# A bias inside 64-token blocks, moved from TensorE matmuls to a POOL multiply behind exp, with the value matmuls one step later

## Chip, core and metric

The kernel runs on one core of a Trainium2 chip. The metric is the device time of one execution in microseconds (us), lower is better. The kernel before takes 1742.46 us (median of 3 runs, 1741.09 to 1747.34).

## What is computed

Four stages in float32 on x of 8 batches x 512 tokens x 128, each followed by a residual sum and a layernorm: an attention with 16 heads of width 8 and a linear distance bias (the first attention), a gated feed-forward with blockwise FP4 rounding of tokens and weights, a second attention without bias, and a local-attention transformer of two layers. The change is in the first attention:

```
slopes = 2 ** (8 * arange(0, -H, -1) / H)                 # one per head, H = 16
scores = einsum('bhqd,bhkd->bhqk', q, k) / sqrt(Hd)
bias   = -slopes[:, None, None] * abs(pos[None, :] - pos[:, None])
probs  = softmax(scores + bias[None], axis=-1)
out    = einsum('bhqk,bhkd->bhqd', probs, v)
```

The second attention has the same form without `bias`.

## The kernel before

**Units and steps.** `attention` is used for both attentions, with `alibi` true for the first. Its work is cut into 32 units, 4 groups of 4 heads in each of 8 batches. A unit has 8 steps in the first pass and 8 in the second; the second pass of a unit lies LAG = 16 steps behind its first. A step `s` thus does one step of the first pass of unit `s // 8` and one of the second pass of unit `(s - 16) // 8`, each for one block of 128 tokens and one pair of heads.

- First pass, in `step`: two matmuls `s_ps` of 128 queries against 512 keys, and VectorE's maximum over the keys into `m` (both heads in one instruction). Two score tiles rotate (pool `p_s`).
- At step 1 of the following unit `shift` transposes the maxima, ScalarE copies them to `mt`, and POOL issues two DMAs that write them into row 63 of q. In this way the second pass subtracts them inside its matmul.
- Second pass, in `step`: two matmuls `t_ps` of 128 keys against 512 queries; ScalarE's exp makes `e` from each (scale: the slope of the head). `t_ps` comes from a pool of three PSUM banks, `p_t`, which transposes and projections share. `e` tiles rotate, 11 of them.
- `values`, two groups of four matmuls for each key block (`part` 0 and 1 are the two halves of the queries), adds up `av` in the only bank of `p_av`. After the last group ScalarE copies `av` to `avs`.
- `divide` transposes `avs` into `o_ps` and divides by the denominator on VectorE. Once in a batch `end_o` and `end_y` transpose and project the output (`ot_ps`, `y_ps`), VectorE makes sum and statistics, and `layernorm` runs six instructions on POOL.

**The bias.** Rows 32 to 47 of the operands q and k carry, for each 64-token block, a signed distance, so that the matmul itself gives the linear bias. For a query in the block of the key this has one sign only, so `corrected` adds, inside the diagonal 64x64 blocks, twice the missing distance: four small bf16 matmuls of the constants `sel` and `tri` into the same bank. It does so in each step for the first pass and for the second.

**What sets the order.** All instructions around the change are kept in program order on their engines. `later(s, f)` puts a function behind `step` number `s`; functions of one step run in the order in which they were put. The due times that matter, with `z` the first step of the second pass of a unit: `values` of block `blk` and half `part` at `z + 2 * blk + 3 + part` (line 413), `divide` at `z + 12` (line 410), `end_o` at `z + 15`, `end_y` with `layernorm` at `z + 18`, `shift` at `n * 8 + 9`. For the next batch's operands `begin_x` runs at 10 steps before a batch's first step, `begin_qk` at 8 and 6 before it (ScalarE's `x`, then POOL's cast and subtraction that make `parts`, then DMAs on the SyncE queue to DRAM and back), `begin_v` and `with_bias` at 20 steps after it. Counted in steps from a batch's start, 58 is thus the one in which `end_y` of that batch, `layernorm` and the second `begin_qk` of the batch after next fall together, in this order. From step 62 on, `quantized_tokens` rounds that batch for the feed-forward (VectorE, POOL and ScalarE).

**Loads.** Weights of the later stages come in `load_weights`, at step 64 of the first attention, among them the local attention's `wqkv_s` (1.5 MB) on the SyncE queue.

Of the kernel before, what the change touches and what calls it, by code (L numbers as in the profile page):

```python
# [9 lines left out]
F32 = mybir.dt.float32  # L10
F32R = mybir.dt.float32r
BF16 = mybir.dt.bfloat16
I32 = mybir.dt.int32
AF = mybir.ActivationFunctionType
ALU = mybir.AluOpType
# [3 lines left out]
P = 128  # L19
B, S, D = 8, 512, 128  # L20
# [5 lines left out]
C_ID, C_TRI, C_SEL, C_MASK0, C_MASK, C_ROT = 0, 128, 256, 512, 640, 768  # L26
# [25 lines left out]
def body(ctx, tc, x, consts, rows, wa0, wa1, acols, bo, wf, wqkv, wo, w1, w2, cols, b2r, qs, ks, out):  # L52
    nc = tc.nc
    pe, dve, act_, pool_ = (Kept(tc, e) for e in (nc.tensor, nc.vector, nc.scalar, nc.gpsimd))
# [5 lines left out]
    cst = outer.tile([P, C_ROT], F32, name="cst")  # L60
# [1 line left out]
    rowq = outer.tile([16, S], F32R, name="rowq")  # L62
    rowk = outer.tile([17, S], F32R, name="rowk")
    sel = outer.tile([P, 2 * P], BF16, name="sel")
    tri = outer.tile([P, P], BF16, name="tri")
    wa = [outer.tile([P, W_ALL], F32, name=f"wa{i}") for i in range(2)]
    wqkv_s = outer.tile([P, 2, 3 * INNER], F32, name="wqkv_s")
    wo_s = outer.tile([P, 2, 4, D], F32, name="wo_s")
# [29 lines left out]
        dve.tensor_copy(rowk, raw[:, 1, :])  # L98
    dve.tensor_tensor(qb, acol[:, :, 0], acol[:, :, 1], ALU.mult)
    dve.tensor_copy(sel, cst[:, C_SEL : C_SEL + 2 * P])  # L100
    dve.tensor_copy(tri, cst[:, C_TRI : C_TRI + P])

    def load_late():
        for b in range(2, B):
# [2 lines left out]
    def load_weights():  # L107
        held(out=cst[:, C_MASK0:C_ROT], in_=consts[:, C_MASK0:C_ROT])
        held(out=wa[1], in_=wa1)
        held(out=wqkv_s, in_=wqkv.rearrange("l p f -> p l f"))  # L110
        held(out=wo_s, in_=wo.rearrange("l (c p) d -> p l c d", p=P))
        held(out=w1_s, in_=w1.rearrange("l p f -> p l f"))
        held(out=w2_s, in_=w2.rearrange("l (c p) d -> p l c d", p=P))
        held(out=cols_s, in_=cols)
# [137 lines left out]
    def attention(li, alibi, qs_, ks_, va, batch, late=None, spare=None, alone=0):  # L252
# [7 lines left out]
        with ExitStack() as st:  # L260
# [1 line left out]
            bank = lambda name: p_t.tile([P, S], F32, tag="t", name=name)  # L262
            begun = len(batch)
            batch += [{} for _ in range(B - begun)]
            work = crow = None

            def hold_o(h):
                h["o"] = work.tile([P, NT, P], F32, tag="o", name="o", bufs=3)
# [2 lines left out]
                for c in range(NT):  # L271
                    pool_.tensor_tensor(xs[:, b * NT + c, :], xn[:, b * NT + c, :], crow, ALU.add)

            def corrected(ps, lo, at, stop):

                for a in range(2):
                    for j in range(2):
                        r = slice(64 * j, 64 * j + 64)
                        mm(
                            ps[j][:, lo + 64 * a : lo + 64 * a + 64], lhsT=sel[r, a * P : (a + 1) * P],  # L280
                            rhs=tri[r, at : at + 64], start=False, stop=stop and a == 1, skip_group_check=True,
                        )

            def step(u, i, v, k):


                if u:
                    blk, pp = i // 2, i % 2
                    p, lo = 2 * u["g"] + pp, (i // 2) * P
                    q, kk = qs_[u["b"] % 2], ks_[u["b"] % 2]  # L290
                    both = p_s.tile([P, 2, S], F32, tag="s", name="s_ps")
                    ps = [both[:, j, :] for j in range(2)]
                    for j in range(2):
                        r = slice(64 * j, 64 * j + 63)
                        mm(
                            ps[j], lhsT=q[r, p, lo : lo + P], rhs=kk[r, p, :], start=True, stop=not alibi,
                            skip_group_check=True,
                        )
                    if alibi:
                        corrected(ps, lo, 0, True)  # L300
                if v:
                    vp, vlo = 2 * v["g"] + k % 2, (k // 2) * P
                    q, kk = qs_[v["b"] % 2], ks_[v["b"] % 2]
                    ts = [bank("t_ps") for j in range(2)]
                    for j in range(2):
                        r = slice(64 * j, 64 * j + 64)
                        mm(
                            ts[j], lhsT=kk[r, vp, vlo : vlo + P], rhs=q[r, vp, :], start=True, stop=not alibi,
                            skip_group_check=True,
                        )  # L310
                if u:
                    if i == 0:
                        u["m"] = small.tile([P, 2, 2, NT], F32, tag="m", name="m")
                    dve.tensor_reduce(u["m"][:, :, pp, blk], both, AX.X, ALU.max)
                if v:
                    if alibi:
                        corrected(ts, vlo, 64, True)
                    for j in range(2):
                        e = work.tile([P, S], F32, tag="e", name="e", bufs=11)
                        act_.activation(e, ts[j], AF.Exp, scale=float(SLOPES[2 * vp + j]) if alibi else 1.0)  # L320
                        v["e"].append(e)

            def shift(u):

# [12 lines left out]
            def values(u, blk, part):  # L337

                if blk == 0 and part == 0:
                    u["av"] = p_av.tile([P, S], F32, tag="av", name="av")  # L340
                at = slice(part * S // 2, (part + 1) * S // 2)
                for r in range(4):
                    mm(
                        u["av"][32 * r : 32 * r + 32, at], lhsT=va[u["b"] % 2][:, blk, 4 * u["g"] + r, :],
                        rhs=u["e"][4 * blk + r][:, at], start=(blk == 0 and part == 0), stop=(blk == NT - 1), skip_group_check=True,
                    )
                if blk == NT - 1 and part == 1:
                    u["avs"] = work.tile([P, S], F32, tag="avs", name="avs")
                    act_.copy(u["avs"], u["av"])

            def divide(u):
# [38 lines left out]
                later(n * NU + 9, shift, units[n])  # L390

            def plan():
                nonlocal work, crow
                const, work = pool("ac", 1), pool("aw", 2)
                dram = pool("ad", 2, space=bass.MemoryType.DRAM)
                begin_x, begin_qk, load_qk, begin_v = operand_steps(
# [7 lines left out]
                for n in range(B * G):  # L404
# [2 lines left out]
                    later(z + 12, divide, units[n])  # L407
                    for blk in range(NT):
                        for part in range(2):
                            later(z + 2 * blk + 3 + part, values, units[n], blk, part)  # L410
                    if g == 0 and begun <= b + 1 < B:

                        early = max(s - 10, 8)
# [13 lines left out]
                if not begun:  # L427
                    begin_x(0, batch[0])
                    begin_qk(0, batch[0], 0, held)
                    begin_qk(0, batch[0], 1, held)  # L430
                    begin_v(0, batch[0])
                    for part in (slice(0, 2), slice(2, 4), 1):
                        load_qk(0, batch[0], 0, part, held)
                        load_qk(0, batch[0], 1, part, held_a)
# [710 lines left out]
    with tc.tile_pool(name="ops", bufs=1) as ops:  # L1145
# [27 lines left out]
        def first_spare(later, done, work, bank, mm, tr, p_s):  # L1173
            temps = lambda: [work.tile([P, S], F32, tag=t, name=t, bufs=1) for t in ("qy", "qm")]
            later(64, load_weights)
            for j in range(3):
                quantize_weights(later, 28 + 11 * j, j, temps, work, bank, tr)

# [53 lines left out]
def _constants():  # L1232
# [1 line left out]
    c = np.zeros((P, C_ALL), np.float32)  # L1234
    c[:, C_ID : C_ID + P] = p == f
    i = p % 64
    c[:, C_TRI : C_TRI + 64] = -2.0 * np.maximum(f[:, 0:64] - i, 0)
    c[:, C_TRI + 64 : C_TRI + P] = -2.0 * np.maximum(i - f[:, 0:64], 0)
    for a in range(2):
        c[:, C_SEL + a * P : C_SEL + (a + 1) * P] = f == 64 * a + i  # L1240
    seen = (f >= i) & (f <= i + 64)
# [16 lines left out]
    at, blk = np.arange(S) - S // 2, np.arange(S) // 64  # L1258
    rows = np.zeros((17, 2, S), np.float32)
    for n in range(8):  # L1260
        sign = np.where(blk <= n, 1.0, -1.0)
        rows[n, 0], rows[8 + n, 0] = blk == n, (blk == n) * at
        rows[n, 1], rows[8 + n, 1] = sign * at, -sign
    rows[16, 1] = -1.0
# [56 lines left out]
```

## Time and profile before

| | us |
|---|---|
| median of 3 runs | 1742.46 |
| profiled execution, device time | 1744.98 |
| its span, first to last instruction | 1743.1 |
| first attention, from its first matmul of scores | about 28 to 505 |
| first feed-forward | about 505 to 620 |
| second attention, the start overlapping the stage before | about 620 to 1020 |
| last stage | about 1020 to 1743 |

Busy time by stage, in us:

| stage | length | TensorE | VectorE | ScalarE | POOL | granted clock |
|---|---|---|---|---|---|---|
| 28 to 505 | 477 | 466.6 | 360.7 | 324.4 | 125.2 | 0.96 |
| 505 to 620 | 115 | 86.6 | 97.1 | 55.7 | 76.0 | 0.96 |
| 620 to 1020 | 400 | 390.4 | 339.5 | 312.3 | 113.7 | 0.98 |

A profile row names engine, line of the kernel, operation, tiles (written <- read), shapes and count. PE is TensorE's matmul, PEld its weight load, DVE VectorE, ACT ScalarE, SP SyncE. Many instructions are issued through helpers, so that they all bear the helper's line (L48, L258, L259); the tile names tell them apart. In square brackets behind a row is how long the engine stood idle before it, and what it waited for. The granted clock is TensorE's, as a share of full speed. Matmuls are pipelined: the distance between two starts says more than the length of one.

### The profile page before, as it was taken

The page shows a single profiled execution, that of the slowest core. Times are in us where ns is not written, and L with a number is a line of the kernel's source. Part 1 is how long each engine was busy: PE and PEld are TensorE (multiplying, and loading weights), DVE is VectorE, ACT ScalarE, POOL GpSimd, SP SyncE. Part 2 cuts the span into 40 slices and gives each one's busy share as a digit, 9 for nine tenths or more (in the row PEclk, how much of TensorE's full clock was granted, in tenths as well). Part 3 has the DMA queues.
Part 4 walks back from the last instruction along what each step waited for, and adds up shares of the span by engine and source line. Part 5 has one row for each costly group of instructions (what it writes and reads, how often), then busy time and mean ns, then how long its engine had stood idle before and what let it go on. Part 6 is the DMA issues. An engine that isn't in the chain of part 4 may idle for free.

```text
span 1743.1 us, 42097 instructions
## 1 busy us (share of the span) xinstructions
PE 1637.8 (94%) x16304; PEld 950.2 (55%) x16305; DVE 1381.6 (79%) x2209; ACT 1257.5 (72%) x2996; POOL 911.9 (52%) x974
## 2 busy tenths in 40 slices
PE   4999999999988789999999989999999999999995
PEld 2455555455546544444444446666766666666664
DVE  4688777878839888888888847788888888888873
ACT  1577777776764558878778867788887888888883
POOL 3223331332126741323222257888888888888873
PEclk7799999999999989999999999999999999999998
DMA  5735222321110234333323101111111111111110
GB/s 125 155 68 143 65 54 47 67 59 26 14 14 1 73 66 84 64 62 73 68 52 55 44 1 35 35 35 38 41 38 35 35 41 38 44 41 42 37 35 25
DMA packets 80777, 90.27 MB, mean 52 GB/s; under 512 B 46097, under 2 KB 58385, under 8 KB 76610
## 3 DMA queue, kind: packets, MB, share of 16 engines
q1 hardware_dynamic: 75504, 85.52, 23.2%
q8 instruction: 130, 2.13, 0.5%
q10 hardware_dynamic: 978, 1.52, 0.3%
q0 software_dynamic: 4096, 0.54, 0.3%
q14 instruction: 69, 0.57, 0.1%
HBM read 41.85 MB, written 18.87 MB: 35 GB/s over the span
## 4 chain that ended last, share of the span: by engine, by line
PE 77%; DVE 7%; ACT 6%; POOL 5%; issue 2%; DMA 2%; SPq 1%; DVEq 0%; POOLq 0%; ACTq 0%
PE av L258 15%; PE s_ps L258 12%; PE t_ps L258 9%; PE y_ps L645 5%; PE sp L645 4%; PE o_ps L645 3%; PE t_ps L645 3%; PE v_ps L645 3%; PE p_ps L645 2%; PE q_ps L645 2%; PE k_ps L645 2%; ACT e L48 2%; PE gp L645 2%; PE ap L645 2%; PE o_ps L259 2%
## 5 line engine op out<-in xcount | busy, mean ns | idle before, releaser
L48 DVE TENSOR_REDUCE m<-s_ps 128x2 f32<-128x1024 f32 x512 | 622.5, 1224 | 154.1 <-PE s_ps L258 148.9
L48 ACT ACTIVATE e<-t_ps 128x512 f32<-128x512 f32 x1024 | 556.3, 596 | 178.4 <-PE t_ps L258 170.1
L258 PE MATMUL av<-e,va 128*32 128x256 f32 x4096 | 328.1, 393 | 10.8 <-ACT avs L48 10.7
L258 PE MATMUL s_ps<-k,q 63*128 63x512 f32 x1024 | 265.3, 511 | 20.5 <-DMA q<-far 14.4
L48 POOL DMA_DIRECT2D q<-mt x128 | 68.9, 542 | 365.9 <-ACT mt L48 365.9
L258 PE MATMUL t_ps<-q,k 64*128 64x512 f32 x1024 | 248.1, 448 | 1.3 <-ACT e L48 1.3
L645 ACT ACTIVATE pw<-sp,m,was_v 128x128 f32<-128x128 f32 x512 | 227.6, 480 | 1.5 <-DVE m L645 1.0
L258 PEld LDWEIGHTS s_ps<-k,q 63*128 63x128 f32 x1024 | 99.8, 189 | 227.9 <-issue 151.3
L645 POOL TENSOR_TENSOR was_v<-was_v 128x16 f32<-128x16 f32 x64 | 187.6, 2931 | 5.3
L258 PEld LDWEIGHTS av<-e,va 128*32 128x32 f32 x4096 | 81.5, 108 | 100.5 <-issue 58.9
L258 PEld LDWEIGHTS t_ps<-q,k 64*128 64x128 f32 x1024 | 122.5, 189 | 22.7 <-ACT e L48 10.6
L645 POOL TENSOR_TENSOR pw<-pw,den 128x1024 f32<-128x1024 f32 x64 | 121.3, 1895 | 9.1 <-DVE den L645 9.1
L645 ACT ACTIVATION_READ_ACCUMULATOR pw<-sp,m,was_v 128x1 f32 x512 | 115.9, 226 | 0.0
L258 PEld LDWEIGHTS <-sel 64*128 64x128 bf16 x2048 | 67.3, 98 | 76.6 <-issue 53.3
L645 DVE TENSOR_REDUCE m<-sp 128x4 f32<-128x512 f32 x128 | 82.2, 683 | 21.9 <-PE sp L645 20.1
L48 POOL CAST parts<-x 128x512 fp32r<-128x512 f32 x32 | 19.5, 610 | 138.4 <-ACT x L48 138.4
L645 POOL TENSOR_TENSOR was_k<-was_k,was_q 128x512 f32<-128x512 f32 x64 | 88.0, 1376 | 6.1 <-DVE was_q L645 6.1
L645 ACT COPY v<-v_ps 128x512 f32<-128x512 f32 x64 | 37.6, 588 | 72.7 <-PE v_ps L645 72.7
L645 PEld LDWEIGHTS t_ps<-cst,was_k 128*128 128x128 f32 x512 | 59.7, 142 | 43.2 <-issue 22.4
L645 DVE COPY pT<-p_ps 128x512 f32<-128x512 f32 x128 | 79.8, 664 | 0.5 <-PE p_ps L645 0.5
L645 PEld LDWEIGHTS p_ps<-cst,pw 128*128 128x128 f32 x512 | 59.8, 141 | 33.0 <-issue 28.0
L645 DVE TENSOR_REDUCE was_v<-was_k 128x16 f32<-128x1024 f32 x64 | 77.0, 1204 | 0.0
(191 smaller groups left out, 3282.1 us busy)
## 6 DMA issues: line engine op xcount, KB each, us to landing
far<-parts SPq DMA_DIRECT2D x64, 256.0 KB
q<-far SPq DMA_DIRECT2D x248, 64.0 KB
k<-far SPq DMA_DIRECT2D x240, 64.0 KB
ve<-v SPq DMA_DIRECT2D x112, 128.0 KB
xn<-in_x SPq DMA_DIRECT2D x8, 256.0 KB
q<-mt POOLq DMA_DIRECT2D x128, 4.0 KB, 3.1
hn<-xs SPq DMA_DIRECT2D x16, 128.0 KB
hn<-xs SPq DMA_DIRECT2D x16, 112.0 KB
```

Of the source, the lines that this page charges most:

```text
L48: return lambda *a, **k: self.tc.keep_in_program_order(f(*a, **k))
L258: mm = lambda *a, **k: tc.keep_in_program_order(nc.tensor.matmul(*a, **k))
L259: tr = lambda *a, **k: tc.keep_in_program_order(nc.tensor.transpose(*a, **k))
L645: kept = lambda f: lambda *a, **k: tc.keep_in_program_order(f(*a, **k))
```

## The change

- The second pass has no corrections any more. Its `t_ps` takes no bias inside a 64-token block: `sign` in the constants is now 0 there.
- `e` becomes one tile for both heads, 6 of them. After the two exps POOL multiplies, in place, the 128 columns of the diagonal block in both heads by a table `near`, exp(-slope x distance) inside a 64-token block and 1 outside.
- `near` (16 heads x 128x128) is made at the start by 16 exps on ScalarE, ahead of the loads of the first batch's k on ScalarE's queue. It lies in the space of `wqkv_s`, whose load moves to step 282, behind the last second-pass step.
- The first pass keeps its four corrections, with one table `tri` of -distance for both sides of the diagonal.
- `values` is due one step later, in both attentions: `z + 2 * blk + 4 + part`. `avs` has one buffer instead of two.

```diff
-    tri = outer.tile([P, P], BF16, name="tri")
+    tri = outer.tile([P, 64], BF16, name="tri")
...
-    dve.tensor_copy(tri, cst[:, C_TRI : C_TRI + P])
+    for j in range(2):
+        r = slice(64 * j, 64 * j + 64)
+        dve.tensor_copy(tri[r], cst[r, C_TRI + 64 * j : C_TRI + 64 * j + 64])
...
-        held(out=wqkv_s, in_=wqkv.rearrange("l p f -> p l f"))
...
                         mm(
-                            ts[j], lhsT=kk[r, vp, vlo : vlo + P], rhs=q[r, vp, :], start=True, stop=not alibi,
+                            ts[j], lhsT=kk[r, vp, vlo : vlo + P], rhs=q[r, vp, :], start=True, stop=True,
                             skip_group_check=True,
                         )
...
                 if v:
+                    e = work.tile([P, 2, S], F32, tag="e", name="e", bufs=6)
+                    for j in range(2):
+                        act_.activation(e[:, j], ts[j], AF.Exp, scale=float(SLOPES[2 * vp + j]) if alibi else 1.0)
+                        v["e"].append(e[:, j])
                     if alibi:
-                        corrected(ts, vlo, 64, True)
-                    for j in range(2):
-                        e = work.tile([P, S], F32, tag="e", name="e", bufs=11)
-                        act_.activation(e, ts[j], AF.Exp, scale=float(SLOPES[2 * vp + j]) if alibi else 1.0)
-                        v["e"].append(e)
+
+                        at = e[:, :, vlo : vlo + P]
+                        pool_.tensor_tensor(at, at, near[:, 2 * vp : 2 * vp + 2, :], ALU.mult)
...
-                    u["avs"] = work.tile([P, S], F32, tag="avs", name="avs")
+                    u["avs"] = work.tile([P, S], F32, tag="avs", name="avs", bufs=1)
...
-                            later(z + 2 * blk + 3 + part, values, units[n], blk, part)
+                            later(z + 2 * blk + 4 + part, values, units[n], blk, part)
...
                     begin_v(0, batch[0])
+                    if alibi:
+
+                        near = wqkv_s.rearrange("p l f -> p (l f)")[:, 0 : 16 * P].rearrange("p (n f) -> p n f", n=16)
+                        for n in range(16):
+                            act_.activation(near[:, n, :], cst[:, C_TRI : C_TRI + P], AF.Exp, scale=float(SLOPES[n]))
...
             later(64, load_weights)
+            later(done(B - 1) - 4, lambda: held(out=wqkv_s, in_=wqkv.rearrange("l p f -> p l f")))
...
-    c[:, C_TRI : C_TRI + 64] = -2.0 * np.maximum(f[:, 0:64] - i, 0)
-    c[:, C_TRI + 64 : C_TRI + P] = -2.0 * np.maximum(i - f[:, 0:64], 0)
+    c[:, C_TRI : C_TRI + P] = np.where(p // 64 == f // 64, -np.abs(f - p), 0)
...
-        sign = np.where(blk <= n, 1.0, -1.0)
+        sign = np.sign(n - blk)
```

## The prediction

> **What bounds the kernel now.** I read the page first, for the busy shares and the chain that ended last. The core is busy on TensorE for 94% of the span, and 77% of the last chain is TensorE.
>
> ```profile
> PE 1637.8 (94%) x16304; PEld 950.2 (55%) x16305; DVE 1381.6 (79%) x2209; ACT 1257.5 (72%) x2996; POOL 911.9 (52%) x974
> PE 77%; DVE 7%; ACT 6%; POOL 5%; issue 2%; DMA 2%; SPq 1%; DVEq 0%; POOLq 0%; ACTq 0%
> ```
>
> Then the windows by stage (columns: window, its length, busy PE, PEld, DVE, ACT, POOL, granted clock, DMA share, GB/s). The first attention runs from about 28 to 505 us, the second from about 620 to 1020. In the middle of the first, TensorE has no idle time, VectorE is at 81% and POOL at 26%:
>
> ```profile
> 350.00:450.00 100.00, 98.88 (x1232) 50.74 (x1231) 80.91 (x102) 71.12 (x137) 26.00 (x38) 1.00 0.19 36
> ```
>
> Last, the timeline of TensorE, for one plain step of the first attention and one of the second, which has no bias and so no corrections (start, length, what):
>
> ```profile
> 214.03 0.49 PE L258 MATMUL s_ps<-k,q 63*128 63x512 f32 x2
> 214.36 0.23 PE L258 MATMUL s_ps<-tri,sel 64*128 64x64 bf16 x4
> 214.43 0.48 PE L258 MATMUL t_ps<-q,k 64*128 64x512 f32 x2
> 214.76 0.23 PE L258 MATMUL t_ps<-tri,sel 64*128 64x64 bf16 x4
> 214.92 0.64 PE L258 MATMUL av<-e,va 128*32 128x256 f32 x8
> 215.49 0.49 PE L258 MATMUL s_ps<-k,q 63*128 63x512 f32 x2
> ```
> ```profile
> 820.23 0.50 PE L258 MATMUL s_ps<-k,q 63*128 63x512 f32 x2
> 820.57 0.40 PE L258 MATMUL t_ps<-q,k 64*128 64x512 f32 x2
> 820.90 0.64 PE L258 MATMUL av<-e,va 128*32 128x256 f32 x8
> 821.47 0.50 PE L258 MATMUL s_ps<-k,q 63*128 63x512 f32 x2
> ```
>
> Starts count, not lengths, since matmuls overlap. First attention: 0.33 to the first pass's correction, 0.07 to the second pass, 0.33 to its correction, 0.16 to the values, 0.57 to the next step: 1.46 us. Second: 0.34, 0.33, 0.57: 1.24 us. A batch (32 steps) of the first takes 57.0 us (POOL's casts of `parts` at 188.65, 245.60, 302.56): 46.8 plain, the rest transposes, projections and short waits, all on TensorE. So TensorE sets the pace here, and a matmul less is time less, until something else is late.
>
> **Removed: the second pass's correction.** 4 matmuls in each of 256 steps: 0.16 each step by the rows, and the second attention confirms that the values then follow `t_ps` at 0.33. 256 x 0.16 = 41.0. About 8 of these steps run at a granted clock of 0.50 (54 to 66 us), where the same four cost about twice as much: 1.3 more. In the last 16 steps, without a first pass, exp paces (1.08 busy, 0.21 waiting for `t_ps`); there the wait goes, 0.05 a step more than counted: 0.8. Sum -43. The new step is 1.31 us; the maximum that VectorE takes in each is 1.23, so VectorE is next in line but not yet the bound.
>
> **Added: POOL's multiply**, 256 of 128x256 f32, both operands in SBUF. No such row; POOL's 128x128 takes 455 ns, its 128x384 840, its 128x512 1060 to 1376. Bounds 0.6 and 0.76; I take 0.66, between 128x128 and 128x384. That is 21 us a batch on an engine that has 15 of 57, so as a rate it is hidden. It lies behind exp and before the values three steps later: exp ends 1.93 us after its step's start, the values of a block's first half want it 0.74 into the third step after, 4.7 us from the start: 2.7 us of slack, of which 0.66 is the multiply. What counts is POOL's order. At the step that ends a batch (58 of each 32, y_ps), POOL's own queue has the layernorm and then the next operand's cast and subtraction:
>
> ```profile
> 307.48 0.24 POOL L48 TENSOR_SCALAR rstd<-stats 128x4 f32<-128x4 f32 x1 [1.96 <-DVE stats L48]
> 307.80 1.04 POOL L48 TENSOR_TENSOR rstd<-rstd,half 128x4 f32<-128x4 f32 x1
> 308.95 3.13 POOL L48 TENSOR_SCALAR xn<-xs,stats,rstd 128x128 f32<-128x128 f32 x4
> 312.04 0.60 POOL L48 CAST parts<-x 128x512 fp32r<-128x512 f32 x1
> 312.73 1.28 POOL L48 TENSOR_TENSOR parts<-x,parts 128x512 fp32r<-128x512 f32 x1
> ```
>
> It waits for `stats`, then runs 6.5 us to 314.0. The multiply of step 59 stands behind that. Moved to the new times (two corrections earlier, 0.32): `stats` at 307.16, POOL free at 313.7, multiply ready at 314.36, at the values with 0.1 of latency 314.45. TensorE is there as follows: step 59 starts at 306.70, 60 at 308.01, 61 at 310.32 (a transpose of 0.59 and the wait below, 0.40), 62 at 311.63, its values at 312.37. Wait 2.08 us, and everything on TensorE is queued behind it. Six batches have both pieces (0 to 5); batch 6 has no next operand and comes out even. +12.5.
>
> A rule of the Trainium skill bears on this wait. TensorE: Matmul & The Clock Gate (What's actually happening) says that the array falls to half clock after one idle window of about 3.4 us. The trace agrees at both ends:
>
> ```profile
> 512.51 2.60 PE L48 MATMUL gu<-wgu,xqT 128*128 128x352 f32 x8 [2.59 <-DVE h L473]
> ...
> 522.48 1.54 PE L473 MATMUL ht_ps<-cst,y 128*128 128x128 f32 x6 [3.69 <-POOL y L473]
> 523.81 4.49 PE L48 MATMUL gu<-wgu,xqT 128*128 128x352 f32 x8
> ```
>
> After 2.59 us idle eight matmuls took 2.60; after 3.69 they took 4.49, and the clock stood at 0.50 until 526. At 2.08 the row and the rule say no loss; past 3.4 the sum would be another one (below).
>
> **Moved: the values a step further behind, in both attentions.** Before, the copy of `av` (`avs`) was made at step 2 of a unit's 8, the next values waited for it in step 3, and the transposes of `divide` came a step later, free of it. Now the copy is at step 3 and `divide`, unmoved, is the first to want it in step 4. Now:
>
> ```profile
> 219.17 0.48 PE L258 MATMUL t_ps<-q,k 64*128 64x512 f32 x2
> ...
> 219.94 0.64 PE L258 MATMUL av<-e,va 128*32 128x256 f32 x8 [0.22 <-ACT avs L48]
> ```
>
> From `t_ps` to the values 0.77 instead of 0.49: 0.28 lost, 0.27 in the second attention; in three units of four (21 waits in 390 us), since the fourth has y_ps in that step. The chain of waits goes exp, `avs`, TensorE: 1.61 us from exp's start. After: exp starts 0.84 into step 3, so `avs` is there at 2.45; the transposes want it at 1.31 + 0.74 = 2.05: 0.40, in all four units. Second attention: 0.77 + 1.62 = 2.39 against 1.24 + 0.67 = 1.91: 0.48. A batch of the first: 4 x 0.40 - 3 x 0.29 = 0.73, of the second 4 x 0.48 - 3 x 0.27 = 1.11; times 8: 5.8 + 8.9 = +14.7. Exp and the next step's matmuls stand behind the same wait.
>
> **FFN tokens' quantization** (steps 63 to 68 of seven batches). VectorE gets 1.39 us there in one step and 0.68 in each of two others, besides 1.23 a step. At 1.46 a step it caught up within the two score buffers; at 1.31 it is late by about 0.65 a batch. ScalarE's 0.65 us `qm` pushes exp and thus `avs` by 0.2. Weight quantization adds about 1 in all. 7 x 0.85 + 1: +7. Here SBUF — State Buffer (Who interferes with whom) speaks against the change: a VectorE instruction with two SBUF inputs is shut out while POOL reads SBUF. Only the two 0.68 us instructions are such (most of their runs stand at 0.68, the longest at 1.55). Shut out by 0.66 each, a batch would lose up to 1.3 more, 9 in all; the maxima read PSUM and are not touched by that rule. I take none of it, as the two rarely meet, and keep 9 for the range.
>
> **Nothing:** 16 exps for the factors lie in ScalarE's gap from 16.05 to 24.16, while it waits to issue k's loads; at 0.3 each (the 16x128 cast takes 0.24) they need 5 of 8 us, and would cost any excess over 8. `tri` in two copies lies beside VectorE's start-up. The weight load of 1.5 MB leaves step 64 for the end: the SyncE queue issues nothing after it until 584.88 and DMA is at 0.00 from 510 to 560; uncovered it would be about 10 us at the 150 GB/s of the first slices. The e buffers (6 pairs for 11 singles) come free a matmul group before they are asked for, as before. The last unit waits for a multiply: +0.6.
>
> **Sum:** -43 + 12.5 + 14.7 + 7 + 0.6 = -8.2, against the profiled execution's 1745.0 (span 1743.1). The median of the runs is 1742.5, 2.5 under it, so 1734.
>
> **Rivals.** (1) The moved wait is absorbed: while TensorE stands, VectorE, which is almost as loaded, catches up, and later waits for it vanish. For it: weight loads of `s_ps` already wait 20.6 us for VectorE in the second attention. Against: a step with the wait is 1.51 against 1.24, all of it visible. 1734 - 14.7 = 1719; 18%. (2) The layernorm doesn't hold the values, since the copies go faster or the wait falls into another: 1734 - 12.5 = 1722; 12%. (3) Slower: the wait behind the layernorm passes 3.4 us and the clock falls. With a multiply of d us it is 2.08 + (d - 0.66) + 2(d - 0.66) - 0.26 (those of 57, 58 and 59; the first 0.26 hidden), 3.4 at d = 1.2. Then each of six batches loses 3.4 plus about 3.4 at half clock (7 us, as from 519 to 529): 41 instead of 12.5, time 1763; 7%. Against it: d would be that of 512 elements. (4) VectorE paces at once, the step stops at 1.39 instead of 1.31: 20 lost, 1754; 5%. That the change doesn't do what it says is excluded on TensorE: the matmuls are gone from the program.
>
> **Numbers.** The likeliest case, all four terms, has 58%, with 1723 to 1746 of its own. Half a per cent, about what a measurement of this kernel can tell from no change, is 8.7 us: faster ends at 1733.7. Half of the likeliest case and rivals 1 and 2 lie below; that gives 0.53, 0.35 and 0.12. Range 1715 to 1752.
>
> **What would show it.** `t_ps<-tri,sel` gone, step 1.31; POOL's multiply at 0.6 to 0.76; the values of step 62 waiting 2 us for POOL, six times; `o_ps` waiting for `avs` 0.4 to 0.5, 64 times; second attention longer by 9 us. Wrong if `o_ps` doesn't wait, if POOL waits spread over more steps than 62, or if the granted clock drops in the first attention.

## The result, and the profile after

The changed kernel takes 1748.16 us (median of 11 runs, 1742.29 to 1749.81); the kernel before took 1741.7 beside it (11 runs, 1739.4 to 1747.34). The ratio is 1.0032, with an interval of 1.0021 to 1.0043: 0.3% slower, where 0.5% faster was forecast. The profiled execution after took 1749.46 us, with a span of 1747.7. Below, one of the four executions of e10 is left out as slow: it took 6414 us at a mean granted clock of 0.23.

The page after, busy shares and the chain that ended last:

```profile
PE 1621.3 (93%) x15280; PEld 915.0 (52%) x15281; DVE 1391.9 (80%) x2210; ACT 1256.5 (72%) x3012; POOL 1096.1 (63%) x1230
...
PE 67%; DVE 10%; ACT 9%; POOL 8%; DMA 3%; issue 2%; SPq 0%; ACTq 0%; POOLq 0%; DVEq 0%
```

The 1024 matmuls are gone (16304 to 15280), but TensorE is only 16.5 us less busy, and its share of the last chain fell from 77% to 67%: VectorE, ScalarE and POOL took over. The window in the middle of the first attention (columns as before):

```profile
350.00:450.00 100.00, 95.61 (x1006) 42.58 (x1008) 83.26 (x103) 70.52 (x139) 67.57 (x97) 1.00 0.16 35
```

In the middle of the first attention TensorE now stands still for 4.4% of the time, against 1.1% before. Below, a "batch" is the distance between the starts of VectorE's maxima, 32 steps on. It was 57.0 us in the first attention and is 57.2; it was 50.1 in the second and is 51.2.

The plain step after, TensorE's timeline (start, length, what):

```profile
220.91 0.50 PE L259 MATMUL s_ps<-k,q 63*128 63x512 f32 x2
221.25 0.23 PE L259 MATMUL s_ps<-tri,sel 64*128 64x64 bf16 x4
221.32 0.48 PE L259 MATMUL t_ps<-q,k 64*128 64x512 f32 x2
221.73 0.64 PE L259 MATMUL av<-e,va 128*32 128x256 f32 x8
222.30 0.50 PE L259 MATMUL s_ps<-k,q 63*128 63x512 f32 x2
```

From `t_ps` to the values it is 0.41 us, not 0.33. The step is 1.39, not 1.31, with nothing waited for in it. Before, `t_ps`, its correction and the values took 0.33 + 0.16 = 0.49. So only 0.08 of the 0.16 came off.

The wait behind the layernorm, on TensorE (step 62 of the second batch):

```profile
192.64 0.50 PE L259 MATMUL s_ps<-k,q 63*128 63x512 f32 x2
...
193.47 0.62 PE L259 MATMUL av<-e,va 128*32 128x256 f32 x4
195.21 0.63 PE L259 MATMUL av<-e,va 128*32 128x256 f32 x4 [1.12 <-POOL e L48]
195.77 0.50 PE L259 MATMUL s_ps<-k,q 63*128 63x512 f32 x2
```

and the same stretch on POOL:

```profile
189.43 3.12 POOL L48 TENSOR_SCALAR xn<-xs,stats,rstd 128x128 f32<-128x128 f32 x4
192.52 0.60 POOL L48 CAST parts<-x 128x512 fp32r<-128x512 f32 x1
193.20 1.27 POOL L48 TENSOR_TENSOR parts<-x,parts 128x512 fp32r<-128x512 f32 x1
194.44 2.78 POOL L48 TENSOR_TENSOR e<-e,wqkv_s 128x256 f32<-128x256 f32 x4
```

Step 62 takes 195.77 - 192.64 = 3.13 us instead of 1.39: the multiply waits for POOL until 194.44 and four of them then follow each other. The wait stands where it was forecast, and costs 1.74 instead of 2.08. It came seven times and not six, and not with one size: step 62 was longer than 1.39 by 2.10 in the first batch, by 1.73 in each of the next four, and by 0.88 in each of the last two, 10.8 us in all. The reason is in the program: the `begin_qk` at step 58 of a batch is not that of the batch after next but of the third one on, so only five batches (0 to 4) have a cast behind their layernorm; in batches 5 and 6 the layernorm alone held the multiply. TensorE's waits in 100 to 490 us of the kernel after (what waits, us in total, times, longest):

```profile
PE o_ps L260 <- ACT avs L48: 9.5, 27, 0.5
PE av L259 <- POOL e L48: 6.5, 7, 1.5
PE s_ps L259 <- DVE m L48: 1.8, 7, 0.3
```

And in 650 to 1000 us, the second attention:

```profile
PE o_ps L260 <- ACT avs L48: 11.5, 28, 0.4
```

In nearly every unit the transposes wait for the copy of `av`, as forecast: 0.35 in the mean in the first attention and 0.41 in the second, where 0.40 and 0.48 were forecast. The group of the multiplies on the page (busy, mean ns of one, idle before):

```profile
L48 POOL TENSOR_TENSOR e<-e,wqkv_s 128x256 f32<-128x256 f32 x256 | 187.0, 736 | 122.1 <-ACT e L48 109.3
```

By stages of the two profiled executions: the first attention (first to last maximum) went from 447.4 to 443.4, of which the first batch alone gained 4.2 (56.1 to 51.9); the second went from 395.4 to 404.3; the rest is within 0.4.

### The profile page after: what moved, and what is told of

The parts are those of the page before. It is cut to its first block, busy times and chain, and to the rows that moved or that the text cites. A ratio compares the mean times of both kernels' runs of the same rounds, so it can differ in the third digit from the quotient of the medians.

```text
span 1747.7 us, 40190 instructions
## 1 busy us (share of the span) xinstructions
PE 1621.3 (93%) x15280; PEld 915.0 (52%) x15281; DVE 1391.9 (80%) x2210; ACT 1256.5 (72%) x3012; POOL 1096.1 (63%) x1230
## 4 chain that ended last, share of the span: by engine, by line
PE 67%; DVE 10%; ACT 9%; POOL 8%; DMA 3%; issue 2%; SPq 0%; ACTq 0%; POOLq 0%; DVEq 0%
PE av L259 12%; PE s_ps L259 10%; PE t_ps L259 7%; PE y_ps L653 5%; PE sp L653 4%; ACT e L48 4%; PE o_ps L653 3%; PE t_ps L653 3%; PE v_ps L653 3%; PE q_ps L653 2%; PE gp L653 2%; PE k_ps L653 2%; PE p_ps L653 2%; DVE m L48 2%; PE ap L653 2%
## 5 line engine op out<-in xcount | busy, mean ns | idle before, releaser
L259 PE MATMUL av<-e,va 128*32 128x256 f32 x4096 | 332.1, 393 | 6.5 <-POOL e L48 6.5
L259 PE MATMUL s_ps<-k,q 63*128 63x512 f32 x1024 | 265.0, 510 | 22.5 <-DMA k<-far 12.5
L48 POOL TENSOR_TENSOR e<-e,wqkv_s 128x256 f32<-128x256 f32 x256 | 187.0, 736 | 122.1 <-ACT e L48 109.3
L653 PE MATMUL y_ps<-wo_s,oT 128*128 128x128 f32 x512 | 74.7, 290 | 0.0
```

What stands on the lines that cost most here:

```text
L48: return lambda *a, **k: self.tc.keep_in_program_order(f(*a, **k))
L259: mm = lambda *a, **k: tc.keep_in_program_order(nc.tensor.matmul(*a, **k))
L653: kept = lambda f: lambda *a, **k: tc.keep_in_program_order(f(*a, **k))
```

## The experiments

Two theories stood for the step. The first: it is 1.39 because POOL's part (its multiply and the later values) stands in the way, and TensorE alone would give 1.31. The second: the four corrections cost TensorE only 0.075 us as work, and twice that where they stand between `s_ps` and `t_ps`; the change removed the cheap group and kept the dear one. Each run is compared with the kernel before on the same chip, whose median was 1743.1 for the first four, 1742.49 for the next four in the order of their numbers, and 1742.45 for the last three.

### The step: e1, e2, e3

**e1**, no multiply on POOL, values at their old step. The kernel leaves out the bias inside a 64-token block in the second pass altogether:

```diff
-                        at = e[:, :, vlo : vlo + P]
-                        pool_.tensor_tensor(at, at, near[:, 2 * vp : 2 * vp + 2, :], ALU.mult)
...
-                            later(z + 2 * blk + 4 + part, values, units[n], blk, part)
+                            later(z + 2 * blk + 3 + part, values, units[n], blk, part)
```

> The changed kernel without POOL's multiply and with the values at their old step: the second pass has no bias inside a block at all (left out), everything else of it is there. Theory A, as predicted: a group of four corrections costs 0.16 us of TensorE, and in the changed kernel POOL or its semaphores hold the values back by 0.08 a step. Then the step here is 1.31 us, a middle batch of the first attention 57.0 - 5.1 = 51.9, the time 1742 - 41 - 2 = 1699. Theory B: the second group was worth only 0.075 us, since t_ps, which stands behind the first pass's group, runs 0.08 longer than in the second attention whatever follows. Then the step is 1.39 as in the changed kernel, a batch 57.0 - 2.4 = 54.6, the time 1742 - 20 - 2 = 1720.

Measured: 1719.35 us, ratio 0.9865 (0.9847 to 0.9884); a batch of 54.4. Its plain step on TensorE:

```profile
216.36 0.50 PE L259 MATMUL s_ps<-k,q 63*128 63x512 f32 x2
216.70 0.23 PE L259 MATMUL s_ps<-tri,sel 64*128 64x64 bf16 x4
216.77 0.48 PE L259 MATMUL t_ps<-q,k 64*128 64x512 f32 x2
217.18 0.64 PE L259 MATMUL av<-e,va 128*32 128x256 f32 x8
217.75 0.50 PE L259 MATMUL s_ps<-k,q 63*128 63x512 f32 x2
```

It is 1.39 again, row by row, without any POOL work in the path. The first theory falls. e1 is also the whole price of the second pass's corrections: 23.8 us of 1743, not 43. (Its middle batches give 8 x 2.65 = 21; single first batches scatter by some us, see the last section.)

**e2**, from e1, with the corrections in the second pass and none in the first:

```diff
-                    if alibi:
-                        corrected(ps, lo)
...
-                            ts[j], lhsT=kk[r, vp, vlo : vlo + P], rhs=q[r, vp, :], start=True, stop=True,
+                            ts[j], lhsT=kk[r, vp, vlo : vlo + P], rhs=q[r, vp, :], start=True, stop=not alibi,
...
+                    if alibi:
+                        corrected(ts, vlo)
```

> The other group alone: the first pass without its corrections (the maximum is taken without the bias inside a block, an upper bound for the same softmax), the second pass with its four, no multiply, values at their old step. Theory B1: a group costs 0.075 of array time, and 0.075 more where the weights of t_ps come after it, because they can't be loaded ahead past it; then this group alone costs 0.075: step 1.31, batch 57.0 - 32 x 0.15 = 52.2, time about 1702. Theory B2: the first group of a step costs 0.15 and a second one 0.075, wherever they stand: step 1.39, batch 54.6, time about 1720. Theory A: 1.40, and the same time as B2 within 2.

Measured: 1714.78 us, ratio 0.9849 (0.9826 to 0.9872); a batch of 53.3. As many matmuls as in e1, behind `t_ps` instead of ahead of it:

```profile
221.71 0.50 PE L259 MATMUL s_ps<-k,q 63*128 63x512 f32 x2
222.04 0.40 PE L259 MATMUL t_ps<-q,k 64*128 64x512 f32 x2
222.28 0.23 PE L259 MATMUL t_ps<-tri,sel 64*128 64x64 bf16 x4
222.45 0.64 PE L259 MATMUL av<-e,va 128*32 128x256 f32 x8
223.02 0.50 PE L259 MATMUL s_ps<-k,q 63*128 63x512 f32 x2
```

The step is 1.31. The second theory holds for the step. B2 of the expectation, by which the first group of a step costs 0.15 wherever it stands, asked for 1.39 and falls. Nor is a group dear because it adds into the bank that the matmul just ahead of it writes: it does so here too. The batch came out 1.1 longer than expected. About 0.4 of that went into the copy of `av`: the values waited for it 8.1 us in 21 waits between 100 and 490 us, against 4.9 in 22 in e1, most likely because exp now starts behind four more matmuls and the step is shorter. The rest was not traced.

**e3**, the changed kernel with the first pass's corrections moved behind `t_ps`, nothing else:

```diff
-                    if alibi:
-                        corrected(ps, lo)
                 if v:
...
                 if u:
+                    if alibi:
+                        corrected(ps, lo)
                     if i == 0:
```

> The changed kernel with one thing moved: the first pass's four corrections are issued behind the two t_ps matmuls instead of ahead of them. Theory B1: the weights of t_ps are loaded ahead again, the step goes from 1.39 to 1.31, a batch from 57.2 to about 54.7, the time from 1748 to about 1728; the maximum starts 0.3 later in its step, for which the two score tiles leave 0.4. Theories A and B2: the step stays at 1.39 and the time at 1748, or a little over, for the later maximum.

Measured: 1735.48 us, ratio 0.9961 (0.9946 to 0.9976); a batch of 55.6. The step is 1.31 here too:

```profile
216.80 0.50 PE L259 MATMUL s_ps<-k,q 63*128 63x512 f32 x2
217.14 0.40 PE L259 MATMUL t_ps<-q,k 64*128 64x512 f32 x2
...
218.11 0.50 PE L259 MATMUL s_ps<-k,q 63*128 63x512 f32 x2
```

So the place alone is worth 0.08 a step, with the same matmuls and all of POOL's work. What the place does is seen in TensorE's weight loads. The changed kernel, in the step shown above that starts at 220.91:

```profile
221.25 0.12 PEld L259 LDWEIGHTS <-sel 64*128 64x128 bf16 x4 [0.15 <-issue]
221.29 0.19 PEld L259 LDWEIGHTS t_ps<-q,k 64*128 64x128 f32 x2
```

and e3, in the step that starts at 216.80:

```profile
216.91 0.24 PEld L259 LDWEIGHTS t_ps<-q,k 64*128 64x128 f32 x2
217.37 0.12 PEld L259 LDWEIGHTS <-sel 64*128 64x128 bf16 x4 [0.23 <-issue]
```

With the corrections behind, the weights of `t_ps` are loaded 0.11 us into `s_ps`, and 0.23 later its matmul runs, 0.40 long by its own record. With the corrections ahead, the load comes only behind theirs, 0.38 into the step, 0.03 ahead of its matmul, which is then 0.48 long. TensorE: Matmul & The Clock Gate (The mechanism), of the Trainium skill, says that a weight load is pulled ahead of running matmuls where it goes to other rows of the array or into the background weight buffer. The rows fit that reading, with the corrections' loads taking the place. That the late load is the reason for the 0.08 is thus a reading of the rows and not shown by a run of its own: no run here shows the buffer itself, and the rule has no price for it. What the runs show is that the place decides: 0.08 us a step.

In e3 less came through than the step gave (1.6 a batch of 2.6). The values of step 62 now stand in front of the same POOL earlier: they waited 9.2 us in 7 waits, longest 1.9, against 6.5 and 1.5. In a middle batch step 62 lost 2.10 (3.41 - 1.31) instead of 1.73. That is 0.4 of the missing 1.0; waits for VectorE (2.7 us in the stretch, against 1.8) and for `avs` (10.2, against 9.5) make another 0.2, and the rest was not traced.

### The later values: e4, e6

**e4**, the changed kernel, values a step later in the first attention only:

```diff
-                            later(z + 2 * blk + 4 + part, values, units[n], blk, part)
+                            later(z + 2 * blk + (4 if alibi else 3) + part, values, units[n], blk, part)
```

> The changed kernel with the values a step later in the first attention alone. Theory: in the second attention the 1.1 us that a batch became longer (50.1 to 51.2) is the wait of divide's transposes for the copy avs; it goes back to 50.1, o_ps no longer waits for avs there, and the time is 1748 - 9 = 1739. Rival: the longer batch comes from the paired exp tiles, which stay: 51.2 and 1748. The first attention is the same in both, 57.2 a batch.

Measured: 1735.4 us, ratio 0.9959 (0.9942 to 0.9975); the first attention's batch is unchanged at 57.2, the second's is 50.1 again. TensorE's waits there are those of before: 4.1 us for `avs` in 21 waits, instead of 11.5 in 28. The second attention is back at 395.5 us (404.3 in the changed kernel); 2.3 more lie in the first batch (49.6 instead of 51.9) and 3.0 in the last stage, which the edit doesn't touch; the section on the hardware comes back to both. Together they can account for a time below the expected 1739.

**e6**, the kernel before with the values a step later in both attentions and one buffer of `avs`, and nothing else of the change:

```diff
-                        e = work.tile([P, S], F32, tag="e", name="e", bufs=11)
+                        e = work.tile([P, S], F32, tag="e", name="e", bufs=12)
...
-                    u["avs"] = work.tile([P, S], F32, tag="avs", name="avs")
+                    u["avs"] = work.tile([P, S], F32, tag="avs", name="avs", bufs=1)
...
-                            later(z + 2 * blk + 3 + part, values, units[n], blk, part)
+                            later(z + 2 * blk + 4 + part, values, units[n], blk, part)
```

> The kernel before with only the values a step later in both attentions (and the 12 exp tiles that this needs, one avs). Theory: divide's transposes then wait for avs in each unit, 0.7 us more a batch of the first attention and 1.1 of the second: 57.0 to 57.7 and 50.1 to 51.2, time 1742 + 15 = 1757. Rival: later values are free where POOL isn't in the way, the waits take the place of others: 57.0, 50.1 or 51.2 for another reason, time 1742.

Measured: 1751.97 us, ratio 1.0054 (1.0036 to 1.0073); batches of 57.3 and 51.2. The move alone makes the kernel slower. The second attention's 1.1 a batch is exact. The first attention's 0.35 is under the expected 0.7: at a step of 1.46 the transposes wait less for the copy (6.9 us in 27 waits, against 9.5 at 1.39).

### POOL's order: e5, e10

**e5**, the changed kernel with the next operand's second projection, cast and subtraction two steps later, so that they no longer stand between the layernorm and the multiply:

```diff
-                        later(early + 4, begin_qk, b + 1, batch[b + 1], 1)
+                        later(early + 6, begin_qk, b + 1, batch[b + 1], 1)
```

> The changed kernel with the second operand's projection, cast and subtraction two steps later (step 60 instead of 58 of a batch), so that POOL comes to the multiplies of steps 59 and 60 right behind the layernorm. Theory: the values of step 62 no longer wait for POOL; the 1.74 us that the wait costs in each of six batches go: a middle batch 57.2 to 55.5, the time 1748 - 10 = 1738. Rival: the layernorm's own 4.6 us hold the multiplies, or the wait only moves behind the cast to step 64: a batch at 57.2, 1748.

Measured: 1734.6 us, ratio 0.9956 (0.9942 to 0.997); batches alternate between 55.2 and 55.9. Most of the waits for POOL are gone from TensorE, 0.5 us being left of 6.5 between 100 and 490:

```profile
PE av L259 <- POOL e L48: 0.5, 2, 0.3
```

The two that are left are those of batches 5 and 6, which had no cast to move. The batch became 1.3 to 2.0 shorter, about the 1.74 that step 62 had lost. The medians fell by more (14 us) than five such waits; in the profiled execution 3.5 us of the gain lie in the last stage, which the edit doesn't touch.

**e10**, the changed kernel with the values at the old step, so that POOL has one step less:

```diff
-                            later(z + 2 * blk + 4 + part, values, units[n], blk, part)
+                            later(z + 2 * blk + 3 + part, values, units[n], blk, part)
```

> The changed kernel with POOL's multiply but the values at their old step in both attentions: what the later step is worth to POOL. Theory: POOL's multiply has 1.3 us less slack and still fits in the steps without a layernorm; the wait behind the layernorm grows by a step of 1.39 to 3.1 us in six batches, the waits for avs fall back by 0.8 a batch and the second attention by 1.1: batch 57.8, second attention 50.1, time 1748 - 9 + 4 = 1743. Rival: with 3.1 us TensorE's granted clock falls once a batch and costs about 3 more: 1760.

Measured: a ratio of 1.0116 (1.0099 to 1.0133), some 1764 us; batches of 60.7 to 63.0. TensorE's timeline at the end of the second batch:

```profile
201.78 0.63 PE L259 MATMUL av<-e,va 128*32 128x256 f32 x4 [2.88 <-POOL e L48]
...
203.38 1.08 PE L259 MATMUL av<-e,va 128*32 128x256 f32 x8
```

and windows from the second batch's start on (the third column from the right is the granted clock):

```profile
145.00:165.00 20.00, 19.73 (x188) 7.96 (x184) 16.15 (x19) 13.67 (x28) 11.91 (x18) 0.83 0.40 99
...
202.00:205.00 3.00, 3.00 (x24) 0.96 (x20) 1.23 (x1) 1.09 (x2) 1.39 (x3) 0.64 0.70 175
205.00:210.00 5.00, 4.91 (x51) 2.02 (x49) 4.54 (x7) 3.22 (x7) 2.55 (x4) 0.88 0.35 66
```

After 2.88 us idle, the eight value matmuls of the next step took 1.08 instead of 0.64, and the clock was at 0.64 and then 0.88: 0.36 x 3 + 0.12 x 5 = 1.7 us lost. From the same wait a batch earlier (3.2 us) the clock was still at 0.83 over 20 us, 3.4 lost. A batch of e1 (54.4) with the wait of 2.88 and these 5.1 makes 62.4; this batch took 62.7. This is the rival of the falling clock, in another kernel than the one it was written for. It also shows what the later step of the values buys: by the ratios the multiply would cost about 15 us more without it than the change does with it.

### What is late next: e7, e8, e9

**e7** joins e3, e4 and e5 (the corrections behind `t_ps`, the second attention's values at the old step, the cast later):

> The changed kernel with three repairs: first pass's corrections behind t_ps, the cast two steps later, the values a step later in the first attention alone. If the three costs add: a middle batch 57.2 - 2.5 - 1.7 = 53.0, the second attention 50.1, the time 1748 - 9 - 6 x 4.2 - 2 x 2.5 = 1709. Rival: the later maximum and the shorter step make VectorE late, a batch at 54.5 and the time at 1720.

Measured: 1719.32 us, ratio 0.9867 (0.9849 to 0.9885), a batch of 54.3. The gains don't add up: 55.6 in e3 and 55.2 to 55.9 in e5 should have given about 54.0, and 53.0 was expected. Between 100 and 490 us TensorE now waits for VectorE, which is busy for 87.55 of 100 us in the middle:

```profile
PE o_ps L260 <- ACT avs L48: 10.3, 28, 0.8
PE s_ps L259 <- DVE m L48: 6.3, 7, 1.1
```

**e8** is e7 without any correction on TensorE:

```diff
-                    if alibi:
-                        corrected(ps, lo)
```

> As the one with three repairs, but with no correction on TensorE at all: the maximum of the first pass is taken without the bias inside a block (an upper bound, for the same softmax), the multiply on POOL stays. Theory: 32 x 0.075 = 2.4 less a batch, step 1.24, batch 50.6, the time about 1690. Rival: VectorE, with its 1.23 us maximum in a step of 1.24 and 6.9 us of other work a batch (46.3 in all), becomes the bound in stretches: batch 52, time about 1702.

Measured: 1712.36 us, ratio 0.9827 (0.981 to 0.9844), a batch of 53.3. The plain step is 1.24, that of the second attention, so 0.07 more came off each step: 2.2 a batch. Only 1.0 of it arrived. The wait of `o_ps` grew to 13.4 us in 28, 0.48 each, and VectorE's to 6.7 in 12.

**e9** is e8 with the two last halves of a unit's values in one step, so that `avs` is copied a step earlier:

```diff
-                            later(z + 2 * blk + (4 if alibi else 3) + part, values, units[n], blk, part)
+                            later(z + 2 * blk + (4 if alibi else 3) + part * (blk < NT - 1), values, units[n], blk, part)
```

> As the kernel with no correction on TensorE, and the two halves of a unit's last key block issued in one step (step 2 of the next 8 in the first attention, step 1 in the second), so that avs is copied a step before anything wants it. Theory: the waits for avs (0.54 four times a batch in the first attention, 0.27 three times in the second) go: a batch 53.4 - 2.1 = 51.3 and 50.1 - 0.8 = 49.3, the time 1712 - 17 - 6 = 1689. Rival: VectorE, late already at the tokens' quantization, takes over and the waits come back as waits for the maxima: first attention 53, time about 1703.

Measured: 1707.63 us, ratio 0.9797 (0.9781 to 0.9814), batches of 52.6 and 50.3. The wait for `avs` is gone, and another has taken its place. Between 100 and 490 us:

```profile
PE t_ps L259 <- ACT e L48: 9.7, 27, 1.1
PE s_ps L259 <- DVE m L48: 3.7, 7, 0.6
```

The second pass now waits for one of the three banks that exp reads. With a step of 1.24 the replies of several other engines are on the path: of the 23 us that were expected 5 came. The second attention gained nothing (50.3 a batch, 50.1 in e8), although its `avs` is copied earlier too; e11 below suggests that the cast's later place is the reason.

### A version that beats both: e11

e11 is e2 (corrections in the second pass only, no multiply) with e9's last halves in one step. The maximum that the first pass subtracts is then that of the scores without correction. It is never below the true one, and a softmax doesn't depend on what is subtracted.

```diff
-                            later(z + 2 * blk + 3 + part, values, units[n], blk, part)
+                            later(z + 2 * blk + 3 + part * (blk < NT - 1), values, units[n], blk, part)
```

> No POOL multiply: the kernel with the second pass's correction alone on TensorE (the maximum taken without the bias inside a block, an upper bound for the same softmax), values at their old step, and the two halves of a unit's last key block in one step. Theory: against the run without the last edit (1715) the waits for avs go, 0.39 three times a batch in the first attention and 0.27 three times in the second: 53.3 to 52.1 and 50.1 to 49.3, time 1715 - 9 - 6 = 1700. Rival: VectorE's lateness takes their place: 1712.

Measured: 1698.54 us (1697.62 to 1699.58), ratio 0.9742 (0.9728 to 0.9757), batches of 51.9 and 49.4. It keeps 1024 small matmuls on TensorE and is 44 us faster than before; e9, with none of them, is 35 us faster. The two differ in more than the corrections: e9 also has POOL's multiply, the values of the first attention a step later, and the cast later. In the second attention the cast's place is the only difference, and there e9 is about 4.6 us longer. The waits of e11 between 100 and 490 us:

```profile
PE t_ps L259 <- ACT e L48: 3.7, 16, 0.5
...
PE s_ps L259 <- DVE m L48: 0.3, 1, 0.3
```

## Why the prediction was wrong

**The step that failed** is the first: "4 matmuls in each of 256 steps: 0.16 each step by the rows, and the second attention confirms that the values then follow `t_ps` at 0.33." They follow at 0.41. So the removed group was worth 0.075 to 0.08 us a step and not 0.16. The second attention was no control for this step, because it has no corrections ahead of `t_ps` either. The distance from a group to its follower (0.16) was read as the cost of the group, but part of it is the end of `t_ps` that runs beside it. The plain steps of all kernels fit two prices, 0.07 to 0.08 us for a group behind `t_ps` and twice that for one ahead of it:

| corrections in the step | us | where |
|---|---|---|
| none | 1.24 | e8, second attention |
| behind `t_ps` | 1.31 | e2, e3 |
| ahead of `t_ps` | 1.39 | after, e1 |
| both | 1.46 | before |

The terms of the sum, against what the runs gave:

| term | forecast | measured | from |
|---|---|---|---|
| corrections removed | -43 | -24 | e1 against before |
| wait behind the layernorm | +12.5 | +10.8 | step 62, seven times: 2.10 + 4 x 1.73 + 2 x 0.88; e5 takes the first five away |
| later values, first attention | +5.8 | +6.8 | what is left of a batch: 8 x (57.2 - 54.35 of e1 - 1.74 - 0.26 of VectorE's wait) |
| later values, second attention | +8.9 | +8.9 | 404.3 - 395.4; e4 takes it away |
| tokens' quantization | +7 | +1.8 | wait of `s_ps` for VectorE, 7 times |
| sum | -8.2, with +0.6 for the last unit | +4 | +4.6 in the profiled executions, +6.5 by the medians |

The first row misses by 19 us and turns the sign; the others together came to 28 where 35 was forecast, which hid part of it. The 19 are about 256 x 0.075.

- **POOL's multiply**: 736 ns, inside the bounds of 0.6 and 0.76 but nearer to the upper one than the 0.66 that was taken. As a rate it is hidden, as forecast. The wait at step 62 is nonetheless shorter than forecast, most likely because steps of 1.39 bring TensorE there later: e3, with the step of 1.31 that the forecast took, lost 2.10 there, where 2.08 was forecast.
- **Layernorm wait**: right in place and in cause; the size was 1.74 instead of 2.08. The count of six was wrong, five with a cast and two without; that the total comes within 2 us of the forecast is partly luck.
- **Later values**: right in mechanism and in place (`o_ps` waits for `avs` in nearly all units). The size is exact in the second attention, where e4 shows it. In the first it is only a remainder; the waits themselves (9.5 us for `avs` in 390 us, against 4.9 in e1) give 0.7 a batch, 5.7 in all, and e6 at its longer step gave 0.35 a batch.
- **Tokens' quantization**: oversized, with 0.26 a batch instead of 0.85. The forecast was for a step of 1.31, and at 1.39 VectorE has more time to catch up. But the step is not the whole of it: at 1.31, TensorE waited for VectorE 6.3 us in 7 waits in e7, 2.7 in 6 in e3 (in both the maximum also starts later in its step), and only 0.2 in e2. The contention that the forecast kept for its range is there but small: VectorE's `qy<-qm,qy` (128x512), with two inputs in SBUF, took 818 ns in the mean after and 681 before, and 682 and 684 in e1 and e2, which have no multiply on POOL.
- **Nothing**: the 16 exps for the factors (3.29 us from 15.73 on) lie in ScalarE's gap, and the late weight load (at 497 us) has nobody waiting for it; from the first attention's last maximum to the second's first it took 130.0 us before and 129.7 after.
- **Rivals**: 1 and 2 each put a term at nothing, and both terms came. Rival 3's mechanism is real (e10, and once in e3), but at step 62 of the changed kernel the clock stays at 1.00. Rival 4 had the number of the step, 1.39, and a time 6 us off, with the wrong cause: VectorE does not pace that step; it is 83% busy there and TensorE waits for it 1.8 us.

What stays open: 2 us between the sum of the terms and the medians, what makes the dear place dear beyond the reading of the load rows, and why a batch in e5 alternates between 55.2 and 55.9.

## What to carry to other kernels

Price a small group of matmuls by how the start-to-start distance of its two neighbours changes without it, in a step that is otherwise the same; a group's own length, or the distance to its follower, counts time that its neighbours overlap. Before work goes to another engine, try where it stands: here moving four small matmuls behind the next large one gave as much per step as deleting a group did (0.08), with no new engine to wait for, though the waits that were there grew. And a due time that is moved for one loop's sake is charged in every loop that shares the line; here the second attention paid 9 us for a change that it had no part in.

## What the runs showed of the hardware

**The clock fell after less idle time than expected.** In e10 it fell after 2.88 us. In the changed kernel, TensorE's timeline at the start of the feed-forward shows it after 2.52, where the same eight matmuls took 2.60 in the kernel before, after 2.59 us of idle time:

```profile
507.00 5.03 PE L48 MATMUL gu<-wgu,xqT 128*128 128x352 f32 x8 [2.52 <-DVE h L481]
```

The length of the idle time does not decide it. In e3 the wait at step 62 of the first batch, 1.93 us, was followed by 3.4 us at 0.50; after the last two waits of e10 for POOL (2.00 and 1.99) and after one of 3.67 us in e6 the clock stayed at 1.00. The kernel before, too, has a stretch at 0.50 from 616.5 on, around the end of a wait of 2.48 us, beside the two waits that the forecast was read from. So "past 3.4 us" was not a safe bound for rival 3.

Where the idle time lies sorts most of the cases. In each profile, every stretch at 0.50 begins on one grid of 3.41 us and lasts for a whole number of its pieces. Cut along that grid, the changed kernel and then the kernel before (the first column of counts is TensorE's busy time, the third column from the right the clock):

```profile
502.79:506.20 3.41, 1.38 (x10) 1.14 (x10) 1.84 (x9) 1.34 (x4) 0.00 (x0) 1.00 0.49 115
506.20:509.61 3.41, 2.61 (x5) 1.64 (x6) 2.46 (x5) 0.00 (x0) 3.14 (x5) 0.50 0.01 2
...
507.29:510.70 3.41, 1.96 (x15) 1.49 (x13) 0.92 (x3) 1.49 (x4) 0.00 (x0) 1.00 0.26 34
510.70:514.11 3.41, 1.59 (x6) 1.10 (x7) 3.08 (x13) 0.32 (x2) 2.20 (x4) 1.00 0.01 2
514.11:517.50 3.39, 2.79 (x11) 1.68 (x10) 2.66 (x5) 1.05 (x3) 3.22 (x5) 1.00 0.00 0
```

After, most of the idle time lies in one piece, in which TensorE is busy for 0.40 of the time, and the next piece runs at 0.50. Before, as much idle time is shared by two pieces, busy for 0.57 and 0.47, and the clock stays. Counted in all 13 profiles from 60 to 1000 us, pieces at full clock in which TensorE was busy under 0.40 were followed by 0.50 in 32 of 32 cases, those from 0.40 to 0.56 in 30 of 59, and those above in 3 of 3353. Busy times of matmuls are modelled, so the border is a rough one, and no run was made to test it. TensorE: Matmul & The Clock Gate (What's actually happening) has a window of about 3.4 us that runs free of the program, which agrees with the grid; but it asks for an idle window before the clock falls, and 2.5 us should never fill one. Here the measurement decides: a window that is more than half idle can be enough.

**The first batch depends on the clock.** It took 47.3 to 56.1 us in the kernels profiled here, without an order that follows their edits. Granted clock of the kernel before in that stretch:

```profile
50.00:60.00 10.00, 8.51 (x71) 5.90 (x73) 8.16 (x7) 4.02 (x9) 4.19 (x8) 0.67 1.07 210
60.00:70.00 10.00, 10.00 (x88) 5.30 (x80) 3.90 (x4) 5.09 (x10) 0.90 (x3) 0.65 0.69 193
```

In e6, with as many matmuls, both stretches stood at 1.00 and the batch took 50.9. The 4.2 us that the changed kernel gained in its first batch are thus not its own with any certainty, and single profiles of this kernel differ by some us for this reason alone. The last stage, which no edit touches, adds to that: it took 732.8 to 738.2 us from the second attention's last maximum to the end.
